# Cross-attention of a two-layer perceiver: when the second bank of energies is filled, and by which key groups

## The chip, the cores and the metric

The kernel runs on one core of a Trainium2 chip. A core has TensorE (PE, with its weight loads PEld), VectorE (DVE), ScalarE (ACT), GpSimd (POOL) and SyncE (SP), which here only issues transfers. The metric is the device time of one execution in microseconds (us), lower is better. Before the change it is 1003.3 us, the median of 3 runs (1003.01 to 1004.56).

## The reference, cut to what matters

The program is a perceiver of two layers on x (2 x 256 tokens, 256 channels) and a context (2 x 4096 tokens, 256 channels): cross-attention, attention and a mixture of experts, twice, each with a layer norm and a residual. The change lies in the second layer's cross-attention. It has 16 heads of 16 channels for each of the 2 batches. Queries come from the normed x, keys and values are the context itself. An integer mask (256 x 4096, the same for all heads) removes keys:

```python
energy = q @ k.T                    # per batch and head: 256 queries x 4096 keys
energy = where(mask == 0, -1e20, energy)
attention = softmax(energy / 16)    # over 4096 keys
out = attention @ v                 # 256 x 16, heads joined, then w_out and b_out
```

## The kernel before

**Units and steps.** The stage runs over 32 units, one for each batch and head (`UNITS`), and in each over 8 steps. A unit has two kinds of work. First it needs, for every query, the maximum of the masked energies (`max_mms`, L947 and L953). Then, twelve steps later (`LEAD = 12`), it computes the energies again with keys on the partitions, exponentiates them, masks them and multiplies them by the values. In one turn of the loop the step `T` of one unit's second part stands beside the step `i = T + 12` of a later unit's maxima.

**Row groups.** A head has 16 channels, and two further rows carry the maximum and ones, so a matmul needs only 32 of PE's 128 rows. The 4096 keys of a unit lie in `kbuf` as four groups of 1024 on four row groups. A step's two maxima matmuls use two groups, its energies the other two.

**The maxima.** A step makes 2 matmuls of 512 keys into a tile `pm` of two banks; DVE adds the mask (`maskN`) and reduces it into `mx`. Two such tiles exist (`p_s`). At the end of a unit `reduce_max_of` reduces, transposes, and sends the row to memory (`maxd`, L963) and back into one row of the queries (L964), so that the second energies come out with the maximum subtracted.

**The energies.** Their tiles `pe` are one bank each, two key tiles of 128 keys by 256 queries, and three exist (`p_e`). A step takes two banks, `step_tiles(s)`: key group 2 and 3 in even steps, 0 and 1 in odd ones. Each bank is filled from one group. The four matmuls (L1050) are issued in turn, then ACT exponentiates both banks (L1057) into `e` tiles, of which there are 10.

**The mask of the exponentials** has three forms. Four of a unit's 16 banks get it added beforehand by a bf16 matmul of `maskA` with the identity (L1027); these are the first banks of the odd steps. One is multiplied by DVE (L1035, one step later, through `later`), and eleven by POOL (L1064).

**The values.** Three steps later (`held`) four matmuls (L1087) add a step's two `e` tiles into `pav`, at four column groups. After step 7's, ACT copies it (L972). After every fourth unit two tiles of `p_e` serve to combine and divide four heads (L978, L987).

**Order and queues.** A scheduler orders the instructions of each engine by priority, so maxima matmuls may move ahead of energies. Keys and queries of unit u + 2 are issued on SP's queue at maxima step 3 (L864, L896, L900), the maxima at the end of a unit. Sqrt and Exp tables of ACT are switched by `get_ready` (L94); at the last step ACT computes `sig` (L1068) and then loads the Sqrt table.

The lead: before `T = 0` the loop makes twelve maxima steps alone.

Of the kernel before, what the change touches and what calls it, by code (L numbers as in the profile page):

```python
# [17 lines left out]
P = 128  # L18
# [8 lines left out]
def tile_perceiver(ctx: ExitStack, tc: tile.TileContext, t):  # L27
# [139 lines left out]

    def step_tiles(s):

        return (2 - 2 * (s % 2), 3 - 2 * (s % 2)), s // 2  # L170

    added_tiles = sorted(step_tiles(s)[0][0] * 8 + 2 * step_tiles(s)[1] for s in (1, 3, 5, 7))
    by_vector = [step_tiles(6)[0][0] * 8 + 2 * step_tiles(6)[1]]
    ADDED = {kt: 2 * n for n, kt in enumerate(added_tiles)}
    KEPT = {kt: 2 * n for n, kt in enumerate(k for k in range(0, NKC, 2) if k not in ADDED)}

# [17 lines left out]
    with ExitStack() as es:  # L196
# [115 lines left out]
        def mask_part(i, pp):  # L312
# [8 lines left out]
            elif i == 16:  # L321
                nc.vector.reduce_max(anyq, anyp, axis=AX.X)
                nc.vector.tensor_scalar(anyq, anyq, NEG / 2, None, op0=ALU.is_gt)
                rows = mp.tile([P, 2, P], F32, name="anyrows")
                nc.vector.tensor_copy(rows, bcast(anyq, P))
                pq = pp.tile([P, 2, D], F32, name="ph")
                for qb in range(2):
                    nc.tensor.matmul(
                        pq[:, 0, qb * P : (qb + 1) * P], lhsT=rows[:, qb, :], rhs=ident, start=True, stop=True
                    )  # L330
                    nc.vector.tensor_scalar_mul(maskN[:, qb, :], maskN[:, qb, :], anyq[:, qb : qb + 1])
                nc.vector.tensor_copy(anyb, pq[:, 0, :])
            else:
                kt = 2 * (i - 17)
                mi = mp.tile([P, 512], I32, name="mi", bufs=2)
                v = mi.rearrange("p (n q) -> p n q", q=S)
                nc.scalar.dma_start(v, t["maskT"][kt * P : (kt + 2) * P, :].rearrange("(n p) q -> p n q", p=P))
                rows = anyb.unsqueeze(1).to_broadcast([P, 2, S])

                if kt in ADDED:  # L340
                    dst = maskA[:, ADDED[kt] : ADDED[kt] + 2, :]
                    nc.vector.scalar_tensor_tensor(dst, v, 0.0, rows, op0=ALU.is_equal, op1=ALU.mult)
                    nc.vector.tensor_scalar(dst, dst, NEG, None, op0=ALU.mult)
                else:
                    dst = maskM[:, KEPT[kt] : KEPT[kt] + 2, :]
                    nc.vector.scalar_tensor_tensor(dst, v, 0.0, rows, op0=ALU.is_equal, op1=ALU.mult)
                    nc.vector.tensor_scalar(dst, dst, -1.0, 1.0, op0=ALU.mult, op1=ALU.add)
# [501 lines left out]
    with ExitStack() as es:  # L849
# [8 lines left out]

        def load_keys(u):
            if u >= len(UNITS):  # L860
                return
            b, h = UNITS[u]
            for g in range(4):
                nc.sync.dma_start(  # L864
                    kbuf[u % KEYS][32 * g : 32 * g + 16, :],
                    t["ctxT"][b, 16 * h : 16 * h + 16, g * 1024 : (g + 1) * 1024],
                )
# [8 lines left out]
        for u in range(2):  # L876
            load_keys(u)
            set_ones(u, (nc.sync, nc.gpsimd) if u == 0 else (nc.gpsimd,))
# [10 lines left out]

        def load_queries(u, queues):  # L890
            if u >= len(UNITS):
                return
            b, h = UNITS[u]
            p0 = (h % 8) * 16
            for g in range(4):
                queues[g % len(queues)].dma_start(  # L896
                    q0[32 * g : 32 * g + 16, u % QN, :], xnT[p0 : p0 + 16, h // 8, b * S : (b + 1) * S]
                )
            if u >= QN:
                queues[0].dma_start(  # L900
                    q0[16:P:32, u % QN, :], zerosd.rearrange("a b -> (a b)").unsqueeze(0).to_broadcast([4, S])
                )

        with tc.issue_after(rooted.ins):
            nc.scalar.mul(q0[:, 1:, :], ones[:, 0:1].unsqueeze(2).to_broadcast([P, QN - 1, S]), 0.0)
        load_queries(1, (nc.sync, nc.scalar))
        for i in range(2, KEYS):
# [6 lines left out]
        nc.sync.dma_start(gates, t["L1_ffn_gates"].partition_broadcast(P))  # L914
        p_s = pool(es, "xa_s", 2, PSUM)
        p_e = pool(es, "xa_e", 3, PSUM)
        p_a = pool(es, "xa_a", 1, PSUM)
        pa = p_a.tile([P, S], F32, name="pav")
        ao = xn
        LEAD = 12  # L920
        mxs = {}


        nc.vector.tensor_copy(pad[:, :, 0:16], xn[:, 0:2, 0:16])
        pt = p_e.tile([P, 512], F32, name="pe")[:, 0:S]
        for qb in range(2):
# [5 lines left out]
        nc.vector.tensor_copy(q0[:, 0, :], pt)  # L932

        def max_mms(i):

            u, s = divmod(i, 8)
            b, h = UNITS[u]
            qb, c, gp = s // 4, (s // 2) % 2, s % 2
            if s == 3:
                load_keys(u + 2)  # L940
                load_queries(u + 2, (nc.sync,))
            if s == 0:
                mxs[u] = sm.tile([P, 2, 4], F32, name="mx", bufs=3)
            pm = p_s.tile([P, 2, 512], F32, name="pm")
            for j in range(2):
                g = 2 * gp + j
                nc.tensor.matmul(  # L947
                    pm[:, j, :], lhsT=q0[32 * g : 32 * g + 32, u % QN, qb * P : (qb + 1) * P],
# [9 lines left out]
        def reduce_max_of(u):  # L958
# [3 lines left out]
            nc.vector.transpose(rows.rearrange("p t i -> p (t i)"), mneg.rearrange("p t i -> p (t i)"))  # L962
            nc.sync.dma_start(maxd[u].rearrange("(t n i) -> n t i", t=2, n=4), rows[0:P:32])  # L963
            nc.sync.dma_start(q0[16:P:32, u % QN, :], maxd[u].unsqueeze(0).to_broadcast([4, S]))  # L964
            return last_max

# [44 lines left out]
        held = []  # L1011
        later = []
        done = summed = divided = None
        n_steps = 8 * len(UNITS)
        for T in range(-LEAD, n_steps + 4):
            i = T + LEAD
            tiles = []
            if 0 <= T < n_steps:
                u, s = divmod(T, 8)
                b, h = UNITS[u]  # L1020
                gs, tp = step_tiles(s)
                for g in gs:
                    pe = p_e.tile([P, 512], F32, name="pe")
                    kt = g * 8 + 2 * tp
                    added = kt in ADDED
                    if added:
                        nc.tensor.matmul(  # L1027
                            pe, lhsT=identb, rhs=maskA[:, ADDED[kt] : ADDED[kt] + 2, :].rearrange("p j q -> p (j q)"),
                            start=True, stop=False,
                        )  # L1030
                    tiles.append((g, kt, pe, added))
            if i < n_steps:
# [13 lines left out]
            if tiles:  # L1046
                for j in range(2):
                    for g, kt, pe, added in tiles:
                        k0 = (2 * tp + j) * P
                        nc.tensor.matmul(  # L1050
                            pe[:, j * S : (j + 1) * S], lhsT=kbuf[u % KEYS][32 * g : 32 * g + 32, k0 : k0 + P],
                            rhs=q0[32 * g : 32 * g + 32, u % QN, :], start=not added, stop=(j == 1 or not added),
                        )
                now = []
                for g, kt, pe, added in tiles:
                    e = sm.tile([P, 2, S], F32, name="e", bufs=10)
                    nc.scalar.activation(e.rearrange("p j q -> p (j q)"), pe, AF.Exp, scale=1.0 / 16.0)  # L1057
                    if not added:

                        if kt in by_vector or (i >= n_steps and g == gs[0]):  # L1060
                            later.append((kt, e))
                        else:
                            ei = e.bitcast(I32)
                            nc.gpsimd.tensor_tensor(ei, ei, maskM[:, KEPT[kt] : KEPT[kt] + 2, :], ALU.mult)  # L1064
                    now.append((kt, e))
                if T == n_steps - 1:
# [14 lines left out]
            if len(held) == 3 or (held and not tiles):  # L1081
                hu, hs, ht = held.pop(0)
                hb, hh = UNITS[hu]
                for j in range(2):
                    for m, (kt, e) in enumerate(ht):
                        n = 2 * j + m
                        nc.tensor.matmul(  # L1087
                            pa[32 * n : 32 * n + 32, :], lhsT=V[:, hb * NKC + kt + j, 17 * hh : 17 * hh + 32],
                            rhs=e[:, j, :], start=(hs == 0), stop=(hs == 7),
                        )  # L1090
# [6 lines left out]
            if i % 8 == 7 and i < n_steps:  # L1097
                last_max = reduce_max_of(i // 8)
                if i == 7:
                    with tc.issue_after(last_max.ins):  # L1100
                        for tt in range(NT):
                            nc.vector.tensor_add(x[:, tt, :], x[:, tt, :], bo)


# [439 lines left out]
```

## Time and profile before

| what | value |
|---|---|
| median of 3 runs | 1003.3 us |
| the profiled execution's own time | 1003.61 us |
| its span | 1001.9 us |
| mean granted TensorE clock | 0.956 |
| first and last energies matmul (L1050) start | 341.1 and 851.5 us |
| busy of the span: PE, DVE, ACT, POOL | 94, 55, 40, 56% |
| 356 to 829 us, busy: PE, DVE, ACT, POOL | 473.0, 327.0, 269.4, 424.0 us |

The span runs from the first to the last instruction; the rest of the execution's time lies around it. Rows of a timeline give the start, the length and the engine, then the line of the kernel, the operation, and how many instructions were joined. A matmul in float32 is two instructions, so four appear as eight. A time in square brackets is how long the engine sat idle before, and what ended that. Waits are summed over all instructions of a line: the total, how often, and the longest.

### The profile page before, as it was taken

Reading aid. Unit: us, or ns where it says so; the run is one execution under the profiler, and the core shown is the slowest. Engines: PE = TensorE matmul, PEld = TensorE weight load, DVE = VectorE, ACT = ScalarE, POOL = GpSimd, SP = SyncE. Lnnn points to the kernel's source line nnn. Section 1 sums busy time; section 2 is a strip of 40 time slices with the busy share of each in tenths; the row PEclk is TensorE's granted clock in tenths of the full one; section 3 lists DMA queues with packets and bytes.
Section 4 is the critical chain, followed back from the end, with each engine's and each line's share of the span. In section 5 each row is a group of like instructions: output and inputs, shape, how many; then the busy total and the mean of one; then the engine's idle time right before and its main releaser. Section 6 shows DMA issues by size and latency. Waiting matters only on the chain. (4 is left out here: it accounts for less than half of the span.)

```text
span 1001.9 us, 19028 instructions
## 1 busy us (share of the span) xinstructions
PE 944.2 (94%) x7166; PEld 572.1 (57%) x7166; DVE 553.6 (55%) x1121; ACT 402.0 (40%) x805; POOL 564.4 (56%) x552
## 2 busy tenths in 40 slices
PE   6999987889995999999999999999999999878997
PEld 5888844656662355555555555555555555665455
DVE  3343567522225566766676666766766662375342
ACT  2111256212221155555555555555555555322011
POOL 6322110011025189898888988888888887121830
PEclk9999999899996599999999999999999999997997
DMA  9866400468837100001010010001001000800000
GB/s 303 261 218 212 137 1 2 140 221 284 302 127 154 34 20 26 21 22 29 15 28 22 22 28 16 28 16 28 24 19 28 2 2 2 179 1 0 1 5 16
DMA packets 62511, 75.17 MB, mean 75 GB/s; under 512 B 21164, under 2 KB 49280, under 8 KB 62416
## 3 DMA queue, kind: packets, MB, share of 16 engines
q1 hardware_dynamic: 51240, 58.21, 19.2%
q10 hardware_dynamic: 8824, 10.40, 3.3%
q0 software_dynamic: 2352, 5.30, 2.2%
q8 instruction: 59, 0.97, 0.4%
q14 instruction: 36, 0.29, 0.1%
HBM read 68.79 MB, written 3.05 MB: 72 GB/s over the span
## 5 line engine op out<-in xcount | busy, mean ns | idle before, releaser
L1064 POOL TENSOR_TENSOR e<-e,maskM 128x512 int32<-128x512 int32 x348 | 448.8, 1311 | 88.7 <-ACT e L1057 67.3
L953 DVE CUSTOM_DVE_ANT_1 junk<-pm,maskN 128x1024 f32<-128x1024 f32 x256 | 313.5, 1225 | 162.2 <-PE pe L1050 153.5
L1057 ACT ACTIVATE e<-pe 128x512 f32<-128x512 f32 x512 | 278.0, 595 | 251.0 <-PE pe L1050 251.0
L1050 PE MATMUL pe<-q,keys 32*128 32x256 f32 x2048 | 331.4, 405 | 0.4 <-ACT e L1057 0.4
L947 PE MATMUL pm<-keys,q 32*128 32x512 f32 x1024 | 299.5, 671 | 2.4 <-DVE mx L953 1.8
L1050 PEld LDWEIGHTS pe<-q,keys 32*128 32x128 f32 x2048 | 214.4, 186 | 19.0 <-issue 4.5
L1087 PE MATMUL pav<-e,V 128*32 128x256 f32 x2048 | 163.9, 392 | 0.7 <-POOL e L1064 0.7
L947 PEld LDWEIGHTS pm<-keys,q 32*128 32x128 f32 x1024 | 80.5, 191 | 97.2 <-issue 75.6
L1087 PEld LDWEIGHTS pav<-e,V 128*32 128x32 f32 x2048 | 41.5, 108 | 82.8 <-issue 65.2
L385 PE MATMUL ph<-xnT,ct 128*128 128x256 f32 x256 | 63.0, 391 | 1.5 <-ACT xnT L46 1.5
L214 POOL COPY V<-cn 128x256 f32<-128x256 f32 x64 | 26.3, 458 | 63.2 <-DMA cn<-in_ctx 63.2
L359 PE MATMUL acc<-cn,g 128*128 128x256 f32 x256 | 60.3, 379 | 0.0
L390 ACT ACTIVATE g<-ph 128x512 f32<-128x512 f32 x32 | 19.1, 597 | 92.0 <-PE ph L385 72.4
L385 PEld LDWEIGHTS ph<-xnT,ct 128*128 128x128 f32 x256 | 50.3, 197 | 9.2 <-ACT xnT L46 1.9
L359 PEld LDWEIGHTS acc<-cn,g 128*128 128x128 f32 x256 | 48.6, 190 | 6.6
L1027 PE MATMUL pe<-maskA,identb 128*128 128x512 bf16 x128 | 50.3, 393 | 0.0
L1381 PE MATMUL pp<-proj,xnT 128*128 128x512 f32 x96 | 46.7, 645 | 0.0
L632 POOL DMA_INDIRECT xg<-xnd,slot_token x9 | 8.6, 960 | 66.4 <-PE px L641 45.4
L1027 PEld LDWEIGHTS <-identb 128*128 128x128 bf16 x128 | 12.2, 96 | 53.2 <-issue 53.2
L1395 POOL TENSOR_TENSOR pw<-pw 128x512 f32<-128x512 f32 (+2 forms) x33 | 27.5, 834 | 23.1 <-DVE pw L1386 21.4
L626 PE MATMUL py<-wd,hT 128*128 128x256 f32 x156 | 38.6, 389 | 1.4 <-issue 1.4
L626 PEld LDWEIGHTS py<-wd,hT 128*128 128x128 f32 x156 | 27.8, 189 | 10.5 <-issue 7.8
(392 smaller groups left out, 860.5 us busy)
## 6 DMA issues: line engine op xcount, KB each, us to landing
ct<-in_ctxT SPq DMA_DIRECT2D x8, 1024.0 KB
cn<-in_ctx SPq DMA_DIRECT2D x8, 1024.0 KB
keys<-in_ctxT SPq DMA_DIRECT2D x128, 64.0 KB
wg<-in_L_ffn_we_gate SPq DMA_DIRECT2D x9, 688.0 KB
wu<-in_L_ffn_we_up SPq DMA_DIRECT2D x9, 688.0 KB
wd<-in_L_ffn_we_down SPq DMA_DIRECT2D x9, 640.0 KB
mi<-in_mask ACTq DMA_DIRECT2D x16, 256.0 KB
mi<-in_maskT ACTq DMA_DIRECT2D x16, 256.0 KB
```

The lines of the kernel that those rows point to most:

```text
L359: nc.tensor.matmul(acc[e][qb], lhsT=g[:, j, qb * P : (qb + 1) * P], rhs=cn[:, fc % 8 + j, :], start=(fc + j == 0), stop=(fc + j == NKC - 1),)
L385: nc.tensor.matmul(ph[:, j, :], lhsT=ct[:, k, f0 : f0 + P], rhs=xnT[:, k, e * D : (e + 1) * D], start=(k == 0), stop=(k == 1),)
L626: nc.tensor.matmul(py, lhsT=hT[0:m, c, :], rhs=w[2][0:m, c, :], start=(c == 0), stop=(c == NC6 - 1))
L947: nc.tensor.matmul(pm[:, j, :], lhsT=q0[32 * g : 32 * g + 32, u % QN, qb * P : (qb + 1) * P], rhs=kbuf[u % KEYS][32 * g : 32 * g + 32, c * ...
L953: nc.vector.tensor_tensor_reduce(out=junk, in0=pm, in1=view, scale=1.0, scalar=-3.0e38, op0=ALU.add, op1=ALU.max, accum_out=mxs[u][:, qb, ...
L1027: nc.tensor.matmul(pe, lhsT=identb, rhs=maskA[:, ADDED[kt] : ADDED[kt] + 2, :].rearrange("p j q -> p (j q)"), start=True, stop=False,)
L1050: nc.tensor.matmul(pe[:, j * S : (j + 1) * S], lhsT=kbuf[u % KEYS][32 * g : 32 * g + 32, k0 : k0 + P], rhs=q0[32 * g : 32 * g + 32, u % QN ...
L1057: nc.scalar.activation(e.rearrange("p j q -> p (j q)"), pe, AF.Exp, scale=1.0 / 16.0)
L1064: nc.gpsimd.tensor_tensor(ei, ei, maskM[:, KEPT[kt] : KEPT[kt] + 2, :], ALU.mult)
L1087: nc.tensor.matmul(pa[32 * n : 32 * n + 32, :], lhsT=V[:, hb * NKC + kt + j, 17 * hh : 17 * hh + 32], rhs=e[:, j, :], start=(hs == 0), sto ...
L1381: nc.tensor.matmul(pp[:, hf * 512 : (hf + 1) * 512], lhsT=xnT[:, k, tt * P : (tt + 1) * P], rhs=proj[:, j, k, hf * 512 : (hf + 1) * 512], ...
L1395: nc.gpsimd.tensor_tensor(pw[:, 0:n], pw[:, 0:n], pw[:, n : 2 * n], ALU.add)
```

## The change

A unit's second banks are made differently. In the first bank of a step nothing changes but which key tiles it holds: `first_bank(s)` takes two neighbours of group 2 in even steps and group 0 in odd ones. A second bank now holds one key tile of group 1 and one of group 3 (`second_bank(s)`), and its two halves are written half a step apart: one half at the end of a step, the other in the midst of the next, which uses the other pair of groups. So its exponential and its mask come in the next step too (`open_bank`).

Since two row groups now write one bank, the second half must wait until the first is complete. An empty instruction on SP's queue (`nop`) waits for the first half's matmul, and the second half's matmul waits for it (`behind`).

The other parts:

- Masks: four banks added beforehand as before, two multiplied by DVE (steps 2 and 6 instead of 6 alone), ten by POOL. The mask tiles are loaded in the order of `BANKS`, with a stride where a bank's two key tiles aren't neighbours.
- The lead has a pool of its own (`xa_0`) with four tiles of two banks[...]. It is closed at `T = 0`, when the three pools of before are opened.
- Until `T = 4` the matmuls keep the program's order.
- Transfers on SP keep the program's order all along, and are spread over the steps (`transfers`): keys in maxima steps 3 and 4, queries in 5 to 7, the maxima's row one step after the unit's end and its way back another step later.

```diff
-    def step_tiles(s):
-        return (2 - 2 * (s % 2), 3 - 2 * (s % 2)), s // 2
-    added_tiles = sorted(step_tiles(s)[0][0] * 8 + 2 * step_tiles(s)[1] for s in (1, 3, 5, 7))
-    by_vector = [step_tiles(6)[0][0] * 8 + 2 * step_tiles(6)[1]]
+    def first_bank(s):
+        return 16 * (1 - s % 2) + 2 * (s // 2), 16 * (1 - s % 2) + 2 * (s // 2) + 1
+    def second_bank(s):
+        return 8 + s, 24 + s
+    BANKS = [first_bank(s) for s in range(8)] + [second_bank(s) for s in range(8)]
+    by_vector = [first_bank(s)[0] for s in (2, 6)]
+    ADDED = {first_bank(s)[0]: 2 * n for n, s in enumerate((1, 3, 5, 7))}
+    KEPT = {kt: 2 * n for n, kt in enumerate(b[0] for b in BANKS if b[0] not in ADDED)}
...
-                nc.scalar.dma_start(v, t["maskT"][kt * P : (kt + 2) * P, :].rearrange("(n p) q -> p n q", p=P))
+                nc.scalar.dma_start(v, t["maskT"].rearrange("(n p) q -> p n q", p=P)[:, kt : k1 + 1 : k1 - kt, :])
...
-        p_s = pool(es, "xa_s", 2, PSUM)
-        p_e = pool(es, "xa_e", 3, PSUM)
-        p_a = pool(es, "xa_a", 1, PSUM)
-        pa = p_a.tile([P, S], F32, name="pav")
+        ahead = ExitStack()
+        p_s = pool(ahead, "xa_0", 4, PSUM)
...
+        def place_mm(*args, **kw):
+            mm = nc.tensor.matmul(*args, **kw)
+            if in_order:
+                tc.keep_in_program_order(mm)
+            return mm
...
-            if s == 3:
-                load_keys(u + 2)
-                load_queries(u + 2, (nc.sync,))
...
-            nc.sync.dma_start(maxd[u].rearrange("(t n i) -> n t i", t=2, n=4), rows[0:P:32])
-            nc.sync.dma_start(q0[16:P:32, u % QN, :], maxd[u].unsqueeze(0).to_broadcast([4, S]))
-            return last_max
+            return last_max, rows
+
+        def transfers(i):
+            u, s = divmod(i, 8)
+            if s == 0 and u > 0:
+                yield nc.sync.dma_start(
+                    maxd[u - 1].rearrange("(t n i) -> n t i", t=2, n=4), max_rows.pop(u - 1)[0:P:32]
+                )
+            elif s == 1 and u > 0:
+                yield nc.sync.dma_start(
+                    q0[16:P:32, (u - 1) % QN, :], maxd[u - 1].unsqueeze(0).to_broadcast([4, S])
+                )
+            elif 3 <= s < 5:
+                yield from load_keys(u + 2, ((0, 1), (2, 3))[s - 3])
+            elif s >= 5:
+                yield from load_queries(u + 2, (nc.sync,), ((0,), (1, 2), (3,))[s - 5])
...
+        def behind(later_one, one):
+            tc.add_manual_dep(
+                later_one.ins, one.ins.name,
+                mybir.DependencyInfo(mybir.DependencyClass.Sync, mybir.DependencyReason.DATA), reason="bank",
+            )
+
+        def energies(u, pe, kt, j, added):
+            g, k0 = kt // 8, kt % 8 * P
+            return place_mm(
+                pe[:, j * S : (j + 1) * S], lhsT=kbuf[u % KEYS][32 * g : 32 * g + 32, k0 : k0 + P],
+                rhs=q0[32 * g : 32 * g + 32, u % QN, :], start=not added, stop=(j == 1 or not added),
+            )
+
+        def exponentials(pe, bank, added, on_vector):
+            kt = bank[0]
+            e = sm.tile([P, 2, S], F32, name="e", bufs=EB)
+            nc.scalar.activation(e.rearrange("p j q -> p (j q)"), pe, AF.Exp, scale=1.0 / 16.0)
+            if not added:
+                if on_vector:
+                    later.append((kt, e))
+                else:
+                    ei = e.bitcast(I32)
+                    nc.gpsimd.tensor_tensor(ei, ei, maskM[:, KEPT[kt] : KEPT[kt] + 2, :], ALU.mult)
+            return bank, e
...
         for T in range(-LEAD, n_steps + 4):
             i = T + LEAD
+            if T == 0:
+                ahead.close()
+                p_s = pool(es, "xa_s", 2, PSUM)
+                p_e = pool(es, "xa_e", 3, PSUM)
+                p_a = pool(es, "xa_a", 1, PSUM)
+                pa = p_a.tile([P, S], F32, name="pav")
+            in_order = T < 4
...
             if tiles:
-                for j in range(2):
-                    for g, kt, pe, added in tiles:
-                        k0 = (2 * tp + j) * P
-                        nc.tensor.matmul(
...
+                energies(u, pe, bank[0], 0, added)
+            if open_bank is not None:
+                ou, os, ope, onow, before = open_bank
+                half = os % 2
+                after = energies(ou, ope, second_bank(os)[half], half, False)
+                behind(after, before)
+                onow.append(exponentials(ope, second_bank(os), False, False))
+                open_bank = None
+            if tiles:
+                energies(u, pe, bank[1], 1, added)
+                ope = p_e.tile([P, 512], F32, name="pe")
+                half = 1 - s % 2
+                first_half = energies(u, ope, second_bank(s)[half], half, False)
+                before = tc.keep_in_program_order(nc.sync.nop())
+                behind(before, first_half)
+                now = [exponentials(pe, bank, added, bank[0] in by_vector or i >= n_steps)]
+                open_bank = (u, s, ope, now, before)
...
+            if i <= n_steps + 1:
+                for transfer in transfers(i):
+                    tc.keep_in_program_order(transfer)
```

## The prediction

> **What bounds the kernel now.** I read the page first, then the timeline of one stretch of the cross-attention, then the waits. The page's busy times and costliest groups:
>
> ```profile
> PE 944.2 (94%) x7166; PEld 572.1 (57%) x7166; DVE 553.6 (55%) x1121; ACT 402.0 (40%) x805; POOL 564.4 (56%) x552
> L1064 POOL TENSOR_TENSOR e<-e,maskM 128x512 int32<-128x512 int32 x348 | 448.8, 1311 | 88.7 <-ACT e L1057 67.3
> L953 DVE CUSTOM_DVE_ANT_1 junk<-pm,maskN 128x1024 f32<-128x1024 f32 x256 | 313.5, 1225 | 162.2 <-PE pe L1050 153.5
> L1057 ACT ACTIVATE e<-pe 128x512 f32<-128x512 f32 x512 | 278.0, 595 | 251.0 <-PE pe L1050 251.0
> L1050 PE MATMUL pe<-q,keys 32*128 32x256 f32 x2048 | 331.4, 405 | 0.4 <-ACT e L1057 0.4
> ```
>
> ACT and DVE mostly wait for PE's energies; POOL is the fullest of the others. PE looks busy throughout, but that does not say its time is used well: four row groups run side by side, so one late chain is covered by the busy time of the others. The chain that ended last is followed only back to 854 us, past the stage in question, so it says nothing here. The timeline does (start, length, engine, instructions): a step with an added mask, then one without.
>
> ```profile
> 395.05 0.70 PE L947 MATMUL pm<-keys,q 32*128 32x512 f32 x2
> 395.06 0.70 PE L1050 MATMUL pe<-q,keys 32*128 32x256 f32 x4
> ...
> 395.60 0.60 PE L1050 MATMUL pe<-q,keys 32*128 32x256 f32 x4
> 396.12 0.64 PE L1087 MATMUL pav<-e,V 128*32 128x256 f32 x8
> ...
> 396.36 1.09 ACT L1057 ACTIVATE e<-pe 128x512 f32<-128x512 f32 x2 [1.18 <-PE pe L1050]
> 396.69 0.70 PE L947 MATMUL pm<-keys,q 32*128 32x512 f32 x2
> ...
> 396.71 0.78 PE L1050 MATMUL pe<-q,keys 32*128 32x256 f32 x3
> ...
> 397.24 0.89 PE L1050 MATMUL pe<-q,keys 32*128 32x256 f32 x5
> 398.07 0.64 PE L1087 MATMUL pav<-e,V 128*32 128x256 f32 x8
> ```
>
> From the first maxima matmul to the value matmuls the first step takes 396.12 - 395.05 = 1.07 us, the second 398.07 - 396.69 = 1.38. The weight loads of the second step, in a narrower window, show why:
>
> ```profile
> 396.81 0.40 PEld L1050 LDWEIGHTS pe<-q,keys 32*128 32x128 f32 x3
> 397.01 0.29 PEld L1050 LDWEIGHTS pe<-q,keys 32*128 32x128 f32 x3
> ```
>
> The second bank's chain starts at about 397.0, not 396.71: with three banks it takes the bank whose exponential is the first of ACT's pair (396.36 to 396.90). So 0.30 us is lost per pair of steps, and a pair takes (414.56 - 398.96) / 4 = 3.90. From the step at 356.00 to that at 826.98 there are 119 pairs, 471 us: 464 of pairs and 7 around the seven combinations of four heads.
>
> The start of the stage, on DVE and PE, at a granted clock of 0.50:
>
> ```profile
> 317.14 1.23 DVE L953 CUSTOM_DVE_ANT_1 junk<-pm,maskN 128x1024 f32<-128x1024 f32 x1 [2.43 <-PE pm L947]
> 318.51 1.23 DVE L953 CUSTOM_DVE_ANT_1 junk<-pm,maskN 128x1024 f32<-128x1024 f32 x1
> 320.55 1.22 DVE L953 CUSTOM_DVE_ANT_1 junk<-pm,maskN 128x1024 f32<-128x1024 f32 x1 [0.81 <-PE pm L947]
> ```
>
> With two buffers, maxima come at 1.37 and 2.04 us in turn; 1.37 is DVE's own pitch. And SyncE's queue:
>
> ```profile
> SPq L963 <- DVE mrows L962: 157.4, 23, 13.3
> SPq L864 <- PE pe L1050: 47.7, 44, 2.7
> ```
>
> It stands waiting in front of transfers, on average 6.8 us for the maxima. That was harmless; it matters below.
>
> **What the Trainium skill says.** "PSUM — Partial Sum Buffer", PSUM bank collisions: different row groups must not write one bank at the same time, and software has to order them. That is why the half-filled bank needs a completion wait; before, both halves came from one group, and no run here shows the collision. "TensorE: Matmul & The Clock Gate", Part 3 (The mechanism): matmuls start and end in program order, and loads overlap only between row groups. The trace agrees: the late chain delayed all behind it by its own 0.3. The same page, What's actually happening: about 3.4 us of sustained work raise the clock. Here it stayed at 0.50 from 316 to about 353 with PE counted busy (14.8 of 16 us)[...]. "ScalarE: Activation LUTs", What ACT_TABLE_LOAD costs: 1283 ns for a load; the trace has 1.28 us.
>
> **The change, part by part** (times from the start of a step's maxima matmuls).
>
> *Bank wait.* In the order that the build gives, each step has the first bank's half, the older bank's second half, the first bank's other half, and the new bank's first half: the same four row groups as now, so still 1.07. ACT gets the older bank at 0.55 + 0.16 (its reaction to PE: 396.20 to 396.36) = 0.71 and ends at 1.31; the first bank's exponential runs 1.31 to 1.86. The next unmasked step begins at 1.07 + 0.57 = 1.64; its first half of a new bank, which takes that bank, comes some 0.27 later, at 1.91, against 1.86 + 0.06 for the semaphore. I leave 0.04 per pair for it: 0.26 x 119 = 31 us gained. Ends: nothing left, 36; 0.2 left, 12.
>
> *Combinations.* The combination and division of four heads draw two tiles from the same three banks. Each then waits for the older bank's exponential, at 1.31 + 0.06 instead of 1.07: 0.3, twice, seven times: 4 us lost (0 to 10).
>
> *Relay.* The second half waits for an event on SyncE's queue, which waits for the first half. First halves end at 1.07 and are seen by SP at about 1.2 (DVE reacts within 0.1: pav at 396.12, DVE at 396.22); the event is priced by PE's own event instruction in the trace, 51 ns, and PE's reaction by 60 ns (DVE ends 319.74, load at 319.80): 1.35. It is needed at 1.64 + 0.1: hidden by the value matmuls, with 0.4 to spare, 0.7 before a masked step. Queued behind the second half on PE are the rest of the energies, then ACT and DVE. Five semaphore increments per step on PE instead of three add perhaps 0.05 at the 26 ns each that the TensorE page states (The cost: per-tile semaphore tail). Cost 0, at worst see the rival.
>
> *SP's queue.* Eleven transfers per unit of 0.39 to 0.59 us each (5.7 us in about 14.6) are spread over the steps with at most two, 1.2 us, between relays 1.6 to 2.0 apart. The maxima's write is reached when DVE has the row about 1.7 into its step, ends at 2.3, and the next relay is due at 2.9. The read waits for the write, 1.66 after it (401.87 to 403.53), and fits one step later. It still lands some 2 steps before use. Cost 0.
>
> *Masks.* POOL loses one multiply per unit (11 x 1.31 to 10 x 1.31 = 13.1), DVE gains one (0.69). DVE's unit: 8 x 1.37 + 2 x 0.75 + 0.45 = 12.9. Both stay under PE's 4 x 3.64 = 14.6. Values are needed two steps after the multiply. Gain 0; without that cover, each 0.1 on a unit is 3 us. The strided mask loads have the same rows and lie in the first stage. Cost 0.
>
> *Start.* Four buffers for the lead: twelve maxima at 1.37 from 317.14, plus 1.6 for the residual's bias adds between (329.98 to 331.56): 335.2. The first step, in program order, waits for the last of them; the maxima's transfer lands at about 328.5 + 1.7 + 2 = 332, earlier. Then five steps until the masked step that stands at 356.00. At half clock (2.0 to 2.6 each, 3.5 with values) it stands at 349.4; at full clock from the outset at 343.5. PE is dense from 335 on, so I take a rise after some 5 us: 346.5, 9.5 gained (6.6 to 12.5).
>
> *End.* The last second bank is exponentiated a step later, after the Sqrt table load: ACT 851.8 + 0.92 + 1.28 + 0.2 + 1.28 (Exp again) + 0.55, then POOL 1.3, values, combination. That is 1.5 later than now, though the transposes of wq move under that wait; the unmasked tail steps gain about 0.5. Loss 1 (0 to 3). Reloading Sqrt at L111 lies beside PE's L1143 matmuls.
>
> Sum: 31 - 4 + 9.5 - 1 = 35.5. The profiled execution took 1003.61 (span 1001.9), the median is 1003.3: **968**.
>
> **Rivals.** (1) *The bank wait only moves*: ACT's exponentials now alternate and the new bank's first half waits 0.2 per pair. Against it: ACT is busy 9.3 of 16 us. Gain 12 - 4 + 9.5 - 1: 987. DVE late by up to 0.4 per unit after its two multiplies would land between. (2) *Slower: SyncE delays the relay.* For it: 157 us of waiting in that queue; if the maxima's write is reached before its row is there, all later relays and PE's second halves stand behind. Against it: it is now issued one step after the maxima's last matmul. It decides where a unit loses 35.5 / 31 = 1.15 us; with 2 us late per unit, 1003 + 62 - 35 = 1030. (3) *More gain*: nothing left of the wait, combinations free, clock up early: 36 + 12.5: 955. That the order is not what the text says is excluded by the build.
>
> **How the numbers follow.** Main case 957 to 977: 0.66. Partial gain, 977 to 1001: 0.17. More than the main case: 0.06. Within 0.2% (about what a measurement can tell from no change): 0.03. Slower: 0.08. Faster is thus 0.89. The range runs from 955 to 987, taking in both ends of the pair's remainder with the start; the likeliest case's own is 957 to 977.
>
> **What would show it.** Right: unmasked steps of 1.07 up to the values, pairs near 3.64, ACT's exponentials single, the stage's first energies at about 335, hardly any PE wait for SP. Wrong: PE loads idle for an SP release, SP in long waits before relays, steps at DVE's or POOL's pace, or a clock of 0.50 well past 350.

## The result and the profile after

| | before | after |
|---|---|---|
| median | 1003.28 us (4 runs, 1003.01 to 1004.56) | 1021.13 us (4 runs, 1019.21 to 1022.87) |
| span of the profiled execution | 1001.9 us | 1020.8 us |
| mean granted TensorE clock | 0.956 | 0.953 |

The changed kernel is slower: ratio 1.0175, 95% interval 1.015 to 1.020. The prediction was 968.

The page of the kernel after, first its busy times, then rows of its costliest groups (busy time and mean ns of one, then the idle time before them and what ended most of it). Many operations now have the line of a helper, L939 for the matmuls:

```profile
PE 946.0 (93%) x7166; PEld 577.8 (57%) x7166; DVE 612.0 (60%) x1152; ACT 405.3 (40%) x807; POOL 513.6 (50%) x521
L1061 POOL TENSOR_TENSOR e<-e,maskM 128x512 int32<-128x512 int32 x317 | 398.7, 1272 | 153.0 <-ACT e L1055 152.9
L1055 ACT ACTIVATE e<-pe 128x512 f32<-128x512 f32 x512 | 278.2, 595 | 260.5 <-PE pe L939 169.1
L960 DVE CUSTOM_DVE_ANT_1 junk<-pm,maskN 128x1024 f32<-128x1024 f32 x256 | 311.8, 1218 | 112.1 <-PE pe L939 77.1
L1090 DVE SCALAR_TENSOR_TENSOR e<-e,maskM 128x512 f32<-128x512 f32 x67 | 87.7, 1308 | 19.0 <-ACT e L1055 13.3
```

POOL has less to do and waits longer for ACT, and ACT waits as long as ever for PE. The engines were relieved, but their supply was not. The timeline of a step with an added mask (maxima from 503.31) and one without (from 504.96) shows where the supply stops:

```profile
502.95 1.27 POOL L1061 TENSOR_TENSOR e<-e,maskM 128x512 int32<-128x512 int32 x1 [0.22 <-ACT e L1055]
...
503.31 0.70 PE L939 MATMUL pm<-keys,q 32*128 32x512 f32 x2
...
503.33 0.70 PE L939 MATMUL pe<-q,keys 32*128 32x256 f32 x4
...
503.46 1.30 DVE L1090 SCALAR_TENSOR_TENSOR e<-e,maskM 128x512 f32<-128x512 f32 x1
...
504.39 0.64 PE L939 MATMUL pav<-e,V 128*32 128x256 f32 x8
504.63 1.09 ACT L1055 ACTIVATE e<-pe 128x512 f32<-128x512 f32 x2 [1.27 <-PE pe L939]
...
504.96 0.70 PE L939 MATMUL pm<-keys,q 32*128 32x512 f32 x2
505.28 0.78 PEld L939 LDWEIGHTS pe<-q,keys 32*128 32x128 f32 x8
...
506.28 0.60 ACT L1055 ACTIVATE e<-pe 128x512 f32<-128x512 f32 x1 [0.56 <-PE pm L939]
506.39 0.16 PEld L939 LDWEIGHTS pav<-e,V 128*32 128x32 f32 x8 [0.33 <-issue]
```

ACT still exponentiates two banks together, and starts 1.32 after the step's maxima (504.63 - 503.31, 506.28 - 504.96), though in the first of the two the older bank's second half was started beside them at 503.33. So there the older exponential ends at about 505.23. The next step's first bank takes that bank: its weights are loaded at 505.28, 0.32 after the maxima's. All of the step's energies stand behind, the next older half too. The release in the last ACT row is a hint: "PE pm". ACT doesn't read the maxima, and yet it gets its bank when they end. It is no more than a hint, for such names can mislead: in the kernel before, DVE reads the maxima and no energies, and 153.5 of its 162.2 us of waiting are put down to "PE pe" (the row of L953 in the prediction). Up to the values the step without a mask takes 1.43 (506.39 - 504.96), where it took 1.38 before.

In the undisturbed stretches eight steps take 15.92 where they took 15.60. A unit in which four heads are combined costs 2.25 more than that; before it was 0.86. The waits of one stretch (420 to 820 us: total, how often, longest) name it, L999 for the combination and L1008 for the division:

```profile
PEld pe L1008 <- ACT e L1055: 7.5, 6, 1.3
PEld pe L999 <- ACT e L1055: 7.4, 6, 1.2
```

The start does what it was meant to. DVE's maxima at half clock:

```profile
321.58 1.23 DVE L960 CUSTOM_DVE_ANT_1 junk<-pm,maskN 128x1024 f32<-128x1024 f32 x1 [2.24 <-PE pm L939]
...
322.96 1.23 DVE L960 CUSTOM_DVE_ANT_1 junk<-pm,maskN 128x1024 f32<-128x1024 f32 x1
...
324.70 1.22 DVE L960 CUSTOM_DVE_ANT_1 junk<-pm,maskN 128x1024 f32<-128x1024 f32 x1 [0.52 <-DVE mx L960]
...
326.07 1.22 DVE L960 CUSTOM_DVE_ANT_1 junk<-pm,maskN 128x1024 f32<-128x1024 f32 x1
...
327.44 1.23 DVE L960 CUSTOM_DVE_ANT_1 junk<-pm,maskN 128x1024 f32<-128x1024 f32 x1
```

The eight of a unit come at 1.37, but for one that is 0.37 late. SyncE's own waits in 420 to 850 us have changed too:

```profile
SPq L1117 <- PE pe L939: 272.3, 208, 3.1
```

But for two waits of 0.5 and less it waits for first halves only; the long waits for the maxima's row are gone.

**Where the time went**, from the two traces. From the first maximum to the last combination matmul the stage takes 552.9 (321.58 to 874.50) instead of 538.4 (317.14 to 855.54), 14.5 more. The steady part: 0.32 x 29.75 units = 9.5. Seven combinations: 1.4 x 7 = 9.8. The end, from the last maximum to the last combination: 30.5 instead of 27.4, 3.1. The start, from the first maximum to the seventeenth: 28.9 instead of 38.1, -9.2. That is 13.2 of the 14.5; the other 1.3 lie between the seventeenth maximum and the last and are not placed. A further 4.4 of the span lie ahead of the stage, in a part that the change hardly touches: this execution had a granted clock of 0.80, 0.68 and 0.83 in 160 to 220 us, the one before 1.00, 0.83 and 0.91. In the other runs below, the first maximum stands between 316.1 and 318.3.

### The profile page after: what moved, and what is told of

Read it like the earlier page. It is cut to its first block, busy times and chain, and to the rows that moved or that the text cites. A ratio compares the mean times of both kernels' runs of the same rounds, so it can differ in the third digit from the quotient of the medians.

```text
span 1020.8 us, 19266 instructions
## 1 busy us (share of the span) xinstructions
PE 946.0 (93%) x7166; PEld 577.8 (57%) x7166; DVE 612.0 (60%) x1152; ACT 405.3 (40%) x807; POOL 513.6 (50%) x521
## 5 line engine op out<-in xcount | busy, mean ns | idle before, releaser
L1061 POOL TENSOR_TENSOR e<-e,maskM 128x512 int32<-128x512 int32 x317 | 398.7, 1272 | 153.0 <-ACT e L1055 152.9
L939 PE MATMUL pe<-q,keys 32*128 32x256 f32 x2048 | 298.5, 405 | 0.0
L939 PE MATMUL pm<-keys,q 32*128 32x512 f32 x1024 | 293.0, 667 | 5.4 <-DVE mx L960 4.8
L939 PEld LDWEIGHTS pe<-q,keys 32*128 32x128 f32 x2048 | 184.6, 185 | 18.8 <-ACT e L1055 2.6
L939 PE MATMUL pav<-e,V 128*32 128x256 f32 x2048 | 163.7, 391 | 1.6 <-POOL e L1061 1.6
L939 PEld LDWEIGHTS pm<-keys,q 32*128 32x128 f32 x1024 | 80.0, 190 | 93.5 <-issue 51.0
L1090 DVE SCALAR_TENSOR_TENSOR e<-e,maskM 128x512 f32<-128x512 f32 x67 | 87.7, 1308 | 19.0 <-ACT e L1055 13.3
L939 PEld LDWEIGHTS pav<-e,V 128*32 128x32 f32 x2048 | 41.4, 108 | 83.3 <-issue 62.5
L939 PE MATMUL pe<-maskA,identb 128*128 128x512 bf16 x128 | 50.0, 391 | 0.8 <-ACT e L1055 0.8
L939 PEld LDWEIGHTS <-identb 128*128 128x128 bf16 x128 | 12.2, 96 | 52.9 <-issue 52.9
```

The source lines that it names most:

```text
L939: mm = nc.tensor.matmul(*args, **kw)
L1090: mul = nc.vector.scalar_tensor_tensor(e, e, 3.0e38, maskM[:, KEPT[kt] : KEPT[kt] + 2, :], op0=ALU.min, op1=ALU.mult)
```

## The experiments

The theory after the traces: **the older half ends late because it was issued behind the maxima.** In the step with an added mask it starts beside them, on row groups of its own. But if matmuls end in program order, as the page cited in the prediction says, it can't be reported before two matmuls of 512 columns have ended.

**Both halves ahead.** The kernel after, with the order turned round:

```diff
+            if tiles:
+                energies(u, pe, bank[0], 0, added)
+            if open_bank is not None:
...
+                after = energies(ou, ope, second_bank(os)[half], half, False)
...
             if i < n_steps:
                 max_mms(i)
...
-            if tiles:
-                energies(u, pe, bank[0], 0, added)
-            if open_bank is not None:
...
-                after = energies(ou, ope, second_bank(os)[half], half, False)
...
```

> The kernel after, with the first bank's first half and the older bank's second half issued ahead of the step's two maxima matmuls; nothing else moves. Completion theory (the older bank's end is held back by the 512-column maxima matmuls that stand before it on PE, so ACT still gets both banks together): the older exponential starts about 0.6 after the step's start instead of 1.27, ACT's exponentials come singly, the unmasked step falls from 1.46 to 1.07 up to the values, a pair from 3.98 to 3.6, a unit from 15.92 to 14.4-14.6; combinations also shrink; time 965 to 975. Rival, the relay over SyncE is what makes the older bank late: the second half is now needed 0.57 after the first one's end instead of 0.7, so its wait would show as PE waiting for SP and the time is not below 1021. Rival, something else pairs the exponentials: 1018 to 1023, ACT still in pairs.

Measured: 967.35 us (ratio to before 0.9641, 0.9605 to 0.9676). Its timeline, again a masked step and one without:

```profile
497.63 0.48 PE L939 MATMUL pe<-q,keys 32*128 32x256 f32 x2
...
497.64 0.70 PE L939 MATMUL pm<-keys,q 32*128 32x512 f32 x2
...
498.46 1.08 ACT L1055 ACTIVATE e<-pe 128x512 f32<-128x512 f32 x2 [0.88 <-PE pe L939]
498.70 0.16 PEld L939 LDWEIGHTS pav<-e,V 128*32 128x32 f32 x8 [0.34 <-POOL e L1061]
...
499.27 0.48 PE L939 MATMUL pe<-q,keys 32*128 32x256 f32 x2
...
499.28 0.70 PE L939 MATMUL pm<-keys,q 32*128 32x512 f32 x2
...
500.10 1.09 ACT L1055 ACTIVATE e<-pe 128x512 f32<-128x512 f32 x2 [0.56 <-PE pe L939]
...
500.34 0.64 PE L939 MATMUL pav<-e,V 128*32 128x256 f32 x8
```

The starts on PE are 0.01 apart, as they were 0.02 apart in the kernel after; only the order in the queue differs. ACT gets the older bank 0.83 after the step's start (498.46 - 497.63) instead of 1.32, the step without a mask takes 1.07 up to the values (500.34 - 499.27), a pair 3.61 and a unit 14.44. Two expectations were wrong. ACT was to start at about 0.6. And its exponentials are still recorded in pairs, because the first bank is ready when the older one is done. The pairing was never the fault, only its start. The relay was needed earlier here, and of PE's waits in 400 to 820 us a single one, of 0.4, is put down to it.

Ends of matmuls in a timeline are modelled, but the count of PE's completions is recorded. All of PE's matmuls raise one semaphore, and ACT waits until it has reached a number that includes the maxima. So the older half might have been reported early, and ACT held up only by the number that it waits for. The record decides that: in each of 140 steps in mid-stage, once what is left of the step before has been counted (within 0.12), the next completion is counted 1.13 to 1.15 after the step's first matmul of queries and keys in the kernel after, and at 0.71 with both halves ahead. Nothing of the older half is reported while the maxima are under way.

**One half at a time.** First the older half alone ahead of the maxima:

> The kernel after with the older bank's second half alone moved ahead of the two maxima matmuls; the first bank's first half stays behind them. Completion theory: the place of the older half is all that counts, ACT gets the older bank about 0.84 after the step's start as in the run with both halves moved, pairs of 3.60, 964 to 972. Rival, the gain of that run came from the first bank's earlier half: above 995.

Measured: 970.46 us (ratio 0.9681, 0.9664 to 0.9698), a unit of 14.45. In 400 to 820 us 101 weight loads are put down to the relay here, with 0.41 idle before each. That does not show it to set the pace: with both halves ahead 100 loads have the same 0.41 before them, put down to ACT, and a unit takes as long. Then the first bank's half alone:

> The kernel after with the first bank's first half alone moved ahead of the two maxima matmuls; the older half stays behind them. Completion theory: the older bank is released at 1.3 as in the kernel after, and the wait for its bank now stands at the head of the unmasked step, in front of the maxima too: pairs of 3.98 or more, 1019 to 1045. Rival, the first bank's half is what counts: below 1000.

Measured: 1045.3 us (ratio 1.0419, 1.0403 to 1.0435), just past the far end of what was expected, a unit of 16.89. The weights of an unmasked step show the wait at its head, with the maxima behind:

```profile
499.00 0.18 PEld L939 LDWEIGHTS pe<-q,keys 32*128 32x128 f32 x1 [0.70 <-ACT e L1055]
...
499.01 0.19 PEld L939 LDWEIGHTS pm<-keys,q 32*128 32x128 f32 x2
```

So the older half's place decides, and the first bank's makes things worse unless the older half is moved too.

**Shorter maxima.** The order of the kernel after, but with the maxima's matmuls cut in two, the second pair behind the older half (`between` issues the first bank's half and the older one's):

```diff
-                    pm[:, j, :], lhsT=q0[32 * g : 32 * g + 32, u % QN, qb * P : (qb + 1) * P],
-                    rhs=kbuf[u % KEYS][32 * g : 32 * g + 32, c * 512 : (c + 1) * 512], start=True, stop=True,
+                        pm[:, j, w * 256 : (w + 1) * 256], lhsT=q0[32 * g : 32 * g + 32, u % QN, qb * P : (qb + 1) * P],
+                        rhs=kbuf[u % KEYS][32 * g : 32 * g + 32, k0 : k0 + 256], start=True, stop=True,
...
+            half_mms(0)
+            between()
+            half_mms(1)
```

> The kernel after in its own order (maxima first, then the first bank's half and the older bank's half), but each maxima matmul of 512 columns is cut into two of 256, and the second pair stands behind the older half. Completion theory: what counts is the length of what must end first, so with 256 columns ahead the older exponential starts at about 0.84 after the step's start, as with nothing ahead, and the wait is gone: a pair of 3.60 to 3.75 (the two further weight loads and semaphores may cost some), 967 to 985. Rival, any maxima matmul ahead of the older half holds it back: 3.98 or more, 1019 to 1030.

Measured: 967.9 us (ratio 0.9633, 0.9604 to 0.9662). The first maxima and ACT's exponentials of three steps, PE's and ACT's timelines:

```profile
495.77 0.48 PE L939 MATMUL pm<-keys,q 32*128 32x256 f32 x2
...
497.74 0.48 PE L939 MATMUL pm<-keys,q 32*128 32x256 f32 x2
...
499.38 0.48 PE L939 MATMUL pm<-keys,q 32*128 32x256 f32 x2
```

```profile
496.67 1.09 ACT L1060 ACTIVATE e<-pe 128x512 f32<-128x512 f32 x2 [0.59 <-PE pe L939]
498.61 1.09 ACT L1060 ACTIVATE e<-pe 128x512 f32<-128x512 f32 x2 [0.86 <-PE pe L939]
500.28 1.08 ACT L1060 ACTIVATE e<-pe 128x512 f32<-128x512 f32 x2 [0.58 <-PE pe L939]
```

ACT starts 0.87 to 0.90 after the maxima. So it is the length of what is ahead that delays the release, not that maxima are ahead: 0.83 with none, 0.87 to 0.90 with 256 columns, 1.32 with 512 (the first completion is counted at 0.71, about 0.73 and 1.15). The further loads and semaphores cost nothing that a unit shows (14.45).

**The order without the half-filled bank.** The kernel before, with both first halves, the maxima, both second halves:

> The kernel before (both banks of a step filled by one key group each, in one step, no relay) with the order alone: the first halves of both banks, then the two maxima matmuls, then the second halves. If the order alone gives the gain, pairs fall from 3.90 towards 3.6 and the time to about 970. If the bank that is filled half a step later is needed as well, the second bank still needs a bank whose exponential ends late, its wait now stands ahead of the maxima, and a pair stays at 3.9 or grows: 1000 to 1030.

Measured: 1010.9 us (ratio 1.0096, 1.007 to 1.0122), a unit of 15.76 instead of 15.60. In a step without a mask the first bank's half starts at 510.00, but the maxima only 0.31 later, behind the second bank's first half, which still waits for its bank:

```profile
510.00 0.78 PE L1052 MATMUL pe<-q,keys 32*128 32x256 f32 x2
...
510.31 0.70 PE L947 MATMUL pm<-keys,q 32*128 32x512 f32 x2
```

Neither the order alone nor the later filling alone gains anything in a unit (15.76 and 15.92 against 15.60); together they bring it to 14.44.

**The combinations.** Their two tiles from the maxima's pool, the same edit in both places:

```diff
-            pt = p_e.tile([P, 512], F32, name="pe")[:, 0:S]
+            pt = p_s.tile([P, 2, 512], F32, name="pm")[:, 0, 0:S]
```

> The kernel after, with the tiles that combine and divide four heads taken from the maxima's pool instead of the energies' three banks. If the seven combinations cost 2.25 each because their tiles wait for the exponentials of the energies' banks (trace of the kernel after: PE waits 1.2 there twice), they fall to about 0.8 as before the change, and the time to about 1011. If the cost is the combinations' own work on PE, or moves to the wait for the maxima's buffers, it stays at 1019 to 1023.

Measured: 1016.29 us (median of three, 1013.33 to 1017.54; a fourth, at a granted clock of 0.939, took 1029.0; ratio 1.0106, 1.0064 to 1.0149), between the two forecasts. A unit with a combination costs 1.26 more than one without, instead of 2.25, and the loads for both tiles no longer wait for ACT: they did wait for the energies' exponentials. 7 of the 9.8 were to be had so. The stage became 4.5 shorter, since this execution's start was 2.3 slower than the kernel after's (31.2 from the first maximum to the seventeenth); its clock in 340 to 350 us was 0.65 instead of 0.69, though its stage had begun 5.4 earlier.

**The masks.**

```diff
-    by_vector = [first_bank(s)[0] for s in (2, 6)]
+    by_vector = [first_bank(6)[0]]
```

> The kernel after with one multiply per unit on DVE (step 6 alone) and eleven on POOL, as before the change. If the DVE multiplies, 1.31 each beside POOL's instead of 0.69, only lengthen an engine that waits anyway, nothing changes: 1019 to 1023. If they set the pace of their steps, a unit falls from 15.92 towards 15.6 and the time to about 1011. If POOL's eleventh multiply hurts: above 1023.

Measured: 1021.57 us (ratio 1.0176, 1.0128 to 1.0225), a unit of 15.92. The masks are free in the kernel after.

**The start alone.** The kernel before with the pool of four tiles and the program order until `T = 4`:

> The kernel before with the change's start alone: twelve maxima steps in a pool of four tiles of two banks, matmuls in program order until T = 4; filling of the banks, masks and transfers as before. From the trace of the kernel after (4.7 earlier at the fifth step, though the stage began 4.4 later): 9 faster than before, 994 (992 to 996). Rival, part of the 9 came from the order of the transfers or the new filling: 996 to 1003.

Measured: 998.96 us (7 runs, 994.5 to 999.22; ratio 0.9937, 0.9915 to 0.9959): 4.1 less by the medians, 6.3 by the ratio, not 9. In the trace, which is of the longest of the seven, the lead gains all that was expected: from the first to the seventeenth maximum 28.3 instead of 38.1, and at the last maximum it is 9.0 ahead. The loss comes later. From the last combination matmul to the end this execution takes 150.9, the one before 146.4. Windows over that part (length, busy PE, PEld, DVE, ACT, POOL, then the granted clock), first the kernel before, then this one:

```profile
878.99:908.99 30.00, 21.42 (x86) 16.70 (x85) 23.52 (x52) 6.61 (x14) 6.61 (x7) 0.89 0.00 1
908.99:928.99 20.00, 18.53 (x49) 10.19 (x50) 9.93 (x37) 4.56 (x14) 7.03 (x10) 0.74 0.00 0
928.99:1001.90 72.91, 64.43 (x206) 38.43 (x204) 26.90 (x39) 9.12 (x19) 27.79 (x41) 0.91 0.02 8
```

```profile
870.00:900.00 30.00, 22.90 (x86) 17.63 (x85) 22.37 (x48) 6.39 (x13) 6.63 (x7) 0.83 0.00 1
900.00:920.00 20.00, 17.06 (x47) 9.97 (x48) 10.91 (x41) 4.76 (x14) 5.97 (x8) 0.74 0.00 0
920.00:997.50 77.50, 69.01 (x209) 40.71 (x207) 27.07 (x39) 9.12 (x19) 28.88 (x43) 0.87 0.02 7
```

The same work ran at a lower granted clock. An earlier end of the stage does not bring that by itself: with both halves ahead the stage ended 36 earlier than before, and the rest took 144.9. Over all the traces of this study that last part took 144.5 to 150.9 us, and three of the seven executions here took 994.5 to 996.5, so the loss need not be in each of them.

**The end, and a faster kernel.** At the last step ACT computes `sig` and loads the Sqrt table, and in the kernel after the last second bank comes behind it:

```profile
868.35 0.22 ACT L1124 ACTIVATE sig<-gates 128x16 f32<-128x16 f32 x1
868.58 1.28 ACT L94 ACT_TABLE_LOAD   x1
869.87 0.20 ACT L94 ACTIVATE ready<-eps 128x1 f32<-128x1 f32 x1
870.09 1.28 ACT L1055 ACT_TABLE_LOAD   x1
871.39 0.60 ACT L1055 ACTIVATE e<-pe 128x512 f32<-128x512 f32 x1
```

Both halves ahead of the maxima, the combinations' tiles from `p_s`, and `sig` with the table one step later (`T == n_steps`):

> Both halves ahead of the maxima, and two things more: the combinations' tiles from the maxima's pool, and the last sigmoid with the Sqrt table one step later, behind the last second bank, so that no Exp table is loaded again. A unit with a combination cost 1.6 more than one without when both halves were ahead; from the maxima's pool about 1.0: 4 gained over seven. From the last maximum to the last combination about 1.5 to 2.5 less. Together 967 - 6: 958 to 964. If the combinations only exchange one wait for another, and the table load was covered: 965 to 969.

Measured: 966.79 us (5 runs, ratio 0.9648, 0.963 to 0.9667), not to be told from 967.35. The end is shorter, 28.1 from the last maximum to the last combination instead of 30.0 with both halves ahead alone. A combination costs 1.6, as without the other pool. The combination's tile no longer waits for ACT, the division's still does (7 times, up to 0.7), and what the first one saves is lost again; where, stays open. Last, with the combinations back in the energies' pool, one mask fewer on PE:

```diff
-    ADDED = {first_bank(s)[0]: 2 * n for n, s in enumerate((1, 3, 5, 7))}
+    ADDED = {first_bank(s)[0]: 2 * n for n, s in enumerate((1, 3, 5))}
```

> Both halves ahead of the maxima, the sigmoid and the Sqrt table one step later, and three banks of a unit with the mask added by PE instead of four: POOL multiplies eleven, DVE two. If PE's own work sets the pace once the wait is gone, a unit loses one mask matmul, 0.32, and goes from 14.44 to 14.12; POOL's unit is 11 x 1.27 = 14.0 and just fits: 967 - 10 - 2, 955 to 959. Rival, POOL is late for the values in the steps where it has two multiplies in a row: 963 to 975.

Measured: **957.84 us** (ratio 0.9537, 0.9507 to 0.9568), the fastest of all. Away from the combinations a unit takes 14.12, and four units with one combination 58.4 instead of 59.4. Against both halves ahead alone the steady part is 7.6 shorter, not 10, and the end 2.2. In 430 to 780 us POOL is now busy for 344.2 of 350: it is near its limit, also because 65 of its 347 multiplies start while one of DVE's is under way and take 1.72 instead of 1.27.

## Why the prediction was wrong

**The bank wait is the step that failed.** It let the older half end at 0.55 and ACT start at 0.71. Measured: 1.32. Of the difference, 0.12 is the half's own: 0.55 is where the second pair of energies starts, while the row at 395.06 shows the first halves ending at 0.71, and with nothing ahead ACT starts at 0.83. The other 0.49 are the maxima ahead of it. The order of the step, maxima first, was in front of me, and so was the rule: "TensorE: Matmul & The Clock Gate", Part 3 (The mechanism), says that matmuls are monotone "in start AND end". I used it for the chain that is delayed, not for the end of a matmul that has little to do itself; the runs confirm it, with 0.83, 0.87 to 0.90 and 1.32 by the length of what is ahead. The rest follows: the older exponential ends at 1.92, not 1.31, and the next step wants the bank at 1.65. A wait of 0.30 per pair on the second bank's chain was replaced by one of 0.32 on the first, in front of all energies. So instead of 31 gained 9.5 were lost, 40 of the 53 between forecast and result.

**Combinations**: priced at 0.3, twice, from the same wrong end of the exponential; 4 became 9.8. With the older half ahead a combination costs 1.59, so even there 0.86 + 0.6 would have been too little by a tenth or so.

**Start**: 9.5 predicted, 9.2 in the trace, 9.8 with the start alone. Right within the stage; of the whole time the run that isolates it gained 4 to 6, and in its trace 4.6 went to a lower clock after the stage.

**End**: 1 predicted (0 to 3), 3.1 measured. The reload was in the sum; moving it away gave 1.9.

**Relay and SyncE's queue**: cost 0, right. No wait of PE for SP shows in the kernel after. Where the relay was needed earlier, waits of up to 0.4 are put down to it, one with both halves ahead and 101 with the older alone, and the unit is the same. The semaphore increments that were priced at 26 ns each are recorded 42 apart (the five of the step at 503.31 come from 504.47 to 504.64); the measurement holds, and no cost of it shows in a unit.

**Masks**: no effect on the time, right, but by a wrong price: DVE's multiply takes 1.31, not 0.69 or 0.75, and its unit some 14, not 12.9.

**Rivals.** The first, that the wait only moves, named the right thing and the wrong amount: it gave 0.2 per pair to a bank that in truth waits 0.32, and let ACT alternate. The slower rival, SyncE, did not occur. That the wait could move to a worse place was not among them. The runs with the older half ahead (967 and 970) are what the sum was made for: with both halves ahead the stage is 36.1 shorter than before. That speaks for the other terms, not for the order that was predicted. Of the 17.9 by which the kernel after is slower, some 3.5 beyond the stage's own 14.5 can't be placed by single executions.

## What to carry to other kernels

Here a matmul that started beside a longer one on other row groups was reported only after it, the longer one having been issued first (1.15 instead of 0.71). When a consumer waits for a buffer, try its last producer ahead of the long matmuls in the queue, or cut these. In a trace, look at the release of the waiting engine: if it names an instruction whose output the engine doesn't read, the order of the queue may be the cause, but try it, for in the kernel before such a name ("PE pe" for DVE) meant nothing of the kind. And when a wait is removed by a shift in time, work out the end of the buffer's last reader again before pricing the next user.

## What was not expected of the hardware

DVE's multiply of two tiles in memory and POOL's hold each other up, whichever is second. POOL's takes 1.27 alone; DVE's, which never runs alone in these traces, takes 0.69 when it starts first. As the second one, DVE's takes 1.31 (the median of all 67 in the kernel after) and POOL's 1.67 (of 36 in the kernel before). In the kernel after, DVE starts 0.51 after POOL (502.95 and 503.46 above) and takes 1.30, ending 0.54 after it. In the kernel before, DVE is first and POOL stretched:

```profile
502.10 0.69 DVE L1035 SCALAR_TENSOR_TENSOR e<-e,maskM 128x512 f32<-128x512 f32 x1
...
502.25 1.67 POOL L1064 TENSOR_TENSOR e<-e,maskM 128x512 int32<-128x512 int32 x1 [0.34 <-ACT e L1057]
```

"SBUF — State Buffer", Who interferes with whom, says so of a DVE instruction with two inputs in this memory: the pair of ports that both engines share is locked by the one that starts first, so the order of issue decides who blocks. In these two cases the second one ends 0.54 and 1.13 after the first, about 0.15 less than its own length, so nearly all of it is blocked. A price read from a row is thus the price of that order.

The granted clock differs between executions in parts that no edit here touches, 0.68 to 0.83 in 180 to 200 us. The stage's first maximum stands anywhere from 316.1 to 321.6, and what follows the stage takes 144.5 to 150.9: more than most of the terms that were priced. The clock also rises at different times behind the same lead: in 340 to 350 us it was 0.91 to 0.95 in the kernels with the older half ahead or the maxima cut, and 0.55 to 0.86 in the others. The waits of the first steps seem to keep it low; this was not tried by itself.
